# Where the ELU or sum of a one-head step stands on VectorE's queue, in a four-layer graph attention kernel

## The chip, the cores and the metric

The kernel runs on one core of one Trainium2 chip. The metric is the device time of one execution in microseconds (us). The engines are named as in the profile: PE is TensorE's matmuls, PEld its weight loads, DVE is VectorE, ACT is ScalarE, POOL is GpSimd, and SP is SyncE, whose queue issues all DMAs of the steady part of the run. L472 means line 472 of the kernel before.

## The reference

Sixteen graphs of 1024 nodes with 256 features go through four attention layers over one adjacency matrix. Every layer normalises x, takes the positive part, runs the layer and adds its result to x. Layers 0 and 2 have four heads of 64 features, layers 1 and 3 have one head of 256. Layers 0 to 2 end in an ELU, layer 3 in a plain positive part.

```python
h  = relu(layernorm(x))
Wh = h @ W                                    # per head
e  = leaky_relu(e_src[:, None] + e_dst[None]) # e_src, e_dst: Wh times two vectors
e  = where(adj > 0, e, -inf)
x  = x + elu(softmax(e, -1) @ Wh)             # layer 3: relu in place of elu
```

## The kernel before

**Steps.** A step is one layer of one graph. Four graphs are in flight at a time, and the function order_of_steps interleaves them, so that after the first steps a four-head step and a one-head step alternate. There are 64 steps, numbered n. Each step is cut into eight groups: for a four-head step two groups per head (four blocks of 128 rows each), for a one-head step one block of 128 rows per group. A group is one call of `aggregate` (64 matmuls of a weight tile with the projected features, L472), which ends with ACT copying the PSUM bank to y (L487).

**Weights.** For each head eight weight tiles w of 128 by 1024 are made on DVE by one instruction each (L455), from G (a broadcast row in PSUM), a column and the mask. The pool for w has 18 buffers (WBUFS). The 19th tile of a run of weights must wait until PE has used the first. Weights are emitted ahead of the matmuls: after each group up to six more tiles of a four-head step (`upto`), so a whole head and more may be queued on DVE before PE wants it.

**G.** For each step the column gcol is transposed on PE (L402), copied by ACT to gT (L404), stored to DRAM by SP (L406) and fetched back by SP as a broadcast row for each head (L430, gs). ACT copies gs to PSUM (L441, g).

**Preparation of a later step.** While step n-2 and n-1 run, the pieces of step n's preparation are emitted at planned places: statistics on DVE and POOL, the normalised rows on ACT (L334), a 16-bit split on ACT (L343), a DMA transpose on SP (L345), a merge on ACT (L351), the projection on PE (L376) with its copies by ACT (L378), two exponentials on ACT (L384, L386), the product on POOL (L388), and last gcol (L394, L395), gT and the store. The tuples FOUR, ONE and their like give for each of the 21 pieces the group at which it is emitted, counted from the first group of step n-2. A value of 11 is thus group 3 of the step before n. Entry 18 is the piece `rows`, which makes gT and stores it.

**The end of a step.** `finish(n)` returns pieces with the group of the next step at which each is to be emitted: `divide` (DVE, L508), `scaled` for each half (POOL, L519 and for an ELU L521), `exponential` for each half (ACT, L525, only for layers 0 to 2), `add` for each half (DVE, L531 and POOL, L532 for an ELU; DVE, L539 for layer 3) and, after layer 3, the stores of the output (L542). The list is called `ending` in the main loop. In a group k, pieces with a place below k are emitted ahead of the group's weights and matmuls, pieces with place k right after the matmuls, and then come the heads (`emit_heads`), the preparation pieces and the further weights:

```python
                while ending and ending[0][0] <= k:
                    ending.pop(0)[1]()
                upto = min(done["tiles"] + (6 if per > 1 else 3), done["free"] + WBUFS)
                emit_heads(upto - 1 + (C // 2 if per == 1 and k >= C - 2 else 0))
                if 8 * n + k in later:
                    later[8 * n + k]()
                prepare(8 * n + k)
                emit_tiles(upto)
```

[...] No scheduler reorders them. `slack(n)` says that the step after n has one head. A one-head step that is followed by a four-head step is one for which `slack(n)` is false. There are 29 such steps: 15 of layer 1 and 14 of layer 3.

Of the kernel before, what the change touches and what calls it, by code (L numbers as in the profile page):

```python
# [50 lines left out]
FOUR = (-8, -8, -5, 0, 1, 0, 3, 5, 5, 5, 5, 1, 4, 5, 5, 5, 5, 6, 8, 8, 10)  # L51
SHORT = (-4, -4, -4, 0, 1, 0, 3, 5, 5, 5, 5, 1, 4, 5, 5, 5, 5, 6, 8, 8, 10)
NEXT = (-4, -4, -4, 1, 3, 2, 5, 8, 8, 8, 8, 4, 7, 8, 8, 8, 8, 9, 10, 10, 12)
ONE = (2, 2, 2, 3, 4, 3, 5, 7, 7, 7, 7, 4, 7, 8, 8, 8, 8, 8, 11, 11, 12)
SOON = (0, 0, 0, 1, 2, 1, 3, 4, 4, 5, 5, 2, 5, 6, 6, 7, 7, 7, 8, 8, 10)
FIRST = (-4, -4, -4, -2, -0.9, -1, -1, -0.8, -0.8, -0.8, -0.8, 0, 0, 1, 1, 1, 1, 1, 2, 2, 4)
TIGHT = (4, 4, 4, 5, 6, 5, 7, 8, 8, 8, 8, 6, 8, 9, 9, 9, 9, 9, 10, 10, 12)
# [13 lines left out]
def kernel(ctx: ExitStack, tc: tile.TileContext, x, adj, ws, avs, out):  # L71
# [421 lines left out]
    def finish(n):  # L493

        b, l = steps[n]
        H = LAYERS[l][0]
        D = F // H
        st = state[n]

        def views(half):  # L500
            s = slice(half * HALF, (half + 1) * HALF)
            return (xs[b][:, s, :].rearrange("p c (h d) -> p (c h) d", h=H),
                    st["y"][:, s, :, 0:D].rearrange("p c h d -> p (c h) d"),
                    st["r"][:, s, :].rearrange("p c h -> p (c h)"))

        def divide():
            st["r"] = small.tile([P, C, H], F32, name="r")
            nc.vector.reciprocal(st["r"], st["y"][:, :, :, D])  # L508

        def scaled(half):  # L510
            xh, yh, r = views(half)
            rb = r[:, :, None].to_broadcast([P, HALF * H, D])
            if l < L - 1:

                e = st["e", half] = prep.tile([P, HALF * H, D], F32, name="rows",
                                                    bufs=HBUFS)
                if H > 1 and slack(n):
                    nc.vector.scalar_tensor_tensor(e, yh, 0.0, rb, op0=ALU.min, op1=ALU.mult)  # L518
            nc.gpsimd.tensor_tensor(yh, yh, rb, op=ALU.mult)  # L519
            if l < L - 1 and not (H > 1 and slack(n)):  # L520
                nc.gpsimd.tensor_scalar(e, yh, 0.0, -3.0e38, op0=ALU.min, op1=ALU.max)  # L521

        def exponential(half):
            if l < L - 1:
                nc.scalar.activation(st["e", half], st["e", half], AF.Exp)  # L525

        def add(half):
            xh, yh, r = views(half)
            if l < L - 1:
                e = st["e", half]  # L530
                nc.vector.scalar_tensor_tensor(e, e, -1.0, yh, op0=ALU.add, op1=ALU.max)  # L531
                nc.gpsimd.tensor_add(xh, xh, e)  # L532
                return
            if n == len(steps) - 4:

                nc.gpsimd.tensor_scalar(yh, yh, 0.0, 3.0e38, op0=ALU.max, op1=ALU.min)
                nc.gpsimd.tensor_add(xh, xh, yh)
                return
            nc.vector.scalar_tensor_tensor(xh, yh, 0.0, xh, op0=ALU.max, op1=ALU.add)  # L539

        def store(half):
            nc.sync.dma_start(  # L542
                out=out[b].rearrange("(p c) f -> p c f", p=P)[:, half * HALF:(half + 1) * HALF],
                in_=xs[b][:, half * HALF:(half + 1) * HALF, :])
            if half == 1 and b + STREAMS < B:
                load(b + STREAMS)

        if n == len(steps) - 3:

            def early(half):  # L550
                xh, yh, r = views(half)
                rb = r[:, :, None].to_broadcast([P, HALF * H, D])
                e = st["e", half] = prep.tile([P, HALF * H, D], F32, name="rows", bufs=HBUFS)
                nc.vector.scalar_tensor_tensor(e, yh, 0.0, rb, op0=ALU.min, op1=ALU.mult)  # L554
                if half == 0:
                    exponential(half)
                nc.vector.tensor_tensor(yh, yh, rb, op=ALU.mult)

            def late(half):
                xh, yh, r = views(half)  # L560
                e = st["e", half]
                nc.vector.scalar_tensor_tensor(e, e, -1.0, yh, op0=ALU.add, op1=ALU.max)
                nc.vector.tensor_add(xh, xh, e)

            def begin():
                divide()
                early(0)
                late(0)
                state[-1]["stats"](0)
                early(1)  # L570
                state[-1]["combined"](0)

            def end():
                late(1)
                state[-1]["stats"](1)
                state[-1]["combined"](1)

            return [(-1, begin), (1, lambda: exponential(1)), (1, end)]


        at = (0, 0, 0, 0, 1, 1, 1) if slack(n) and H > 1 else (0, 0, 1, 1, 2, 2, 3)
        return list(zip(at, (divide, lambda: scaled(0), lambda: scaled(1), lambda: exponential(0),
                             lambda: exponential(1), lambda: add(0), lambda: add(1)))) + (
                    [(4, lambda: store(0)), (4, lambda: store(1))] if l == L - 1 else [])
# [86 lines left out]
    with tc.manual_schedule():  # L671
        blocks = [mask_rows(c) for c in range(C)]
        layer = [weight_columns(l) for l in range(L)]
        layer[0][0](nc.scalar)
        load(0, 2)
        load_weights(0)
        for c in range(C):
            blocks[c][0]()
        load(1)
        load_weights(1)  # L680
        for i in range(2, STREAMS):
            load(i)
        for l in range(1, L):
            layer[l][0]()
        nc.scalar.activation(warm, half1, AF.Exp)
        nc.vector.tensor_copy(identb, ident)
        layer[0][1]()
        first = [piece for _, piece in preparation(0)]

        order = (  # L690

            [first[0], first[1], first[3], lambda: layer[0][2](range(1)), first[2],
             lambda: layer[0][2](range(1, K)), first[5], first[6], first[4], layer[0][3]]

            + [blocks[c][1] for c in range(4)]
            + [first[7], first[8], blocks[0][2], blocks[4][1], blocks[5][1], blocks[0][3],
               first[9], first[10], blocks[1][2], blocks[6][1], blocks[7][1], blocks[1][3],
               first[11], first[12], blocks[2][2], blocks[0][4],
               lambda: prepare(-4), first[13], first[14], blocks[1][4], blocks[2][3],
               blocks[3][2], first[15], first[16], blocks[3][3]]  # L700

            + [first[17], blocks[4][2], first[18], first[19], lambda: emit_heads(0),
               blocks[5][2], blocks[6][2], blocks[4][3], blocks[4][4], blocks[5][3], blocks[5][4],
               blocks[6][3], blocks[7][2], blocks[2][4], blocks[3][4], blocks[7][3],
               lambda: prepare(-2), blocks[6][4], lambda: prepare(-1), blocks[7][4]])
        plan(1)
        planned = 2
        done["prepared"] = 1
        for piece in order:
            piece()  # L710
        emit_tiles(C, must=True)
        prepare(-0.5)
        for i in range(2, STREAMS):
            load_weights(i)

        for l, at in ((1, 2), (2, 8 * 3 + 4), (3, 8 * 5 + 4)):
            for i, piece in zip((0, 1, 7), layer[l][1:]):
                later[at + i] = piece
        for n in range(len(steps)):
            for k, (h, i0, per) in enumerate(groups(n)):  # L720
                while planned < len(steps) and min(
                        a[0] for a in agenda_of[planned:planned + 2]) <= 8 * n + k:
                    plan(planned)
                    planned += 1
                while ending and ending[0][0] < k:
                    ending.pop(0)[1]()
                emit_tiles(place[n, h, C - 1] + 1, must=True)
                aggregate(n, h, i0, per)
                if i0 + per == C:
                    done["free"] = place[n, h, C - 1] + 1  # L730
# [5 lines that stand above are left out]
                if 8 * n + k in later:  # L736
                    later[8 * n + k]()
                prepare(8 * n + k)
                emit_tiles(upto)
            for _, piece in ending:  # L740
                piece()
            ending = finish(n) if n < len(steps) - 1 else []
# [35 lines left out]
```

## Time and profile before

| What | us |
|---|---|
| Median of three runs | 2445.25 (2444.63 to 2452.23) |
| The profiled execution's own time | 2449.74 |
| Its span, first to last instruction | 2448.0 |
| PE busy in that span | 2394.8 |
| DVE busy | 2040.0 |
| ACT busy | 1480.0 |
| POOL busy | 1073.7 |
| One pair of a four-head and a one-head step, 1373.96 to 1448.35 | 74.39 |

The page counts the time in which an engine works and the time in which it is idle, with what ended the idle time. The granted TensorE clock was 0.997 of full speed over the span. In the timeline of one engine a line has the start, the busy time, the engine, the source line, the operation, the tiles, and how many instructions were put together, and in square brackets the idle time ahead of it with the instruction that ended it. A wait on PE by DVE at L455 is a weight tile that waits for its buffer. A wait on ACT at L441 by DVE is one for G.

### The profile page before, as it was taken

How to read it: one execution, taken by the hardware profiler on the slowest of the kernel's cores; microseconds unless marked ns; L12 is line 12 of the kernel's file. 1: busy time of each engine (PE TensorE's matmuls, PEld its weight loads, DVE VectorE, ACT ScalarE, POOL GpSimd, SP SyncE). 2: the span in 40 equal slices, each digit the busy share in tenths (PEclk: the TensorE clock that was granted, in tenths of full speed). 3: DMA queues.
4: the chain of work that ended last, by engine and by line, in shares of the span. 5: the costliest groups of instructions: out<-in, count | busy, mean ns of one | idle time of the engine just before them, and what ended most of it. 6: DMA issues, size and time to landing. Idle time of an engine off the chain costs nothing.

```text
span 2448.0 us, 86681 instructions
## 1 busy us (share of the span) xinstructions
PE 2394.8 (98%) x39177; PEld 2153.2 (88%) x39177; DVE 2040.0 (83%) x2141; ACT 1480.0 (60%) x2505; POOL 1073.7 (44%) x1350
## 2 busy tenths in 40 slices
PE   7999999999999999999999999999999999999999
PEld 5888899899888888898998888888988998988987
DVE  8988588898888988887988888888889888888794
ACT  5465676565666656765656765566655577656542
POOL 3345455433345454544433554543443345545331
PEclk9999999999999999999999999999999999999999
DMA  5322233243333222323433322224334323223220
GB/s 182 83 53 63 45 79 67 66 114 92 85 96 79 72 63 52 74 71 96 114 89 88 80 62 71 64 50 108 75 93 114 95 48 80 68 65 76 75 54 35
DMA packets 292220, 191.84 MB, mean 78 GB/s; under 512 B 261778, under 2 KB 264586, under 8 KB 289930
## 3 DMA queue, kind: packets, MB, share of 16 engines
q1 hardware_dynamic: 291840, 186.29, 30.6%
q8 instruction: 307, 5.03, 0.9%
q14 instruction: 63, 0.52, 0.1%
q10 hardware_dynamic: 10, 0.00, 0.0%
HBM read 104.87 MB, written 17.43 MB: 50 GB/s over the span
## 4 chain that ended last, share of the span: by engine, by line
PE 82%; ACT 7%; DMA 5%; DVE 4%; issue 2%; POOL 0%; SPq 0%; DVEq 0%; ACTq 0%
PE bank L472 64%; PE bank L376 17%; DVE w L455 2%; DMA gs<-grow 2%; ACT rows L334 2%; DMA grow<-gT 2%; ACT g L441 1%; ACT rows L343 1%; ACT rows L525 1%; ACT rows L351 1%; ACT y L487 1%; DVE bn L287 1%; DMA rows<-rows 0%; PE bank L402 0%; ACT whx L378 0%
## 5 line engine op out<-in xcount | busy, mean ns | idle before, releaser
L472 PE MATMUL bank<-whx,w 128*64 128x65 f32 x36864 | 1898.0, 240 | 17.9 <-DVE w L455 9.3
L472 PEld LDWEIGHTS bank<-whx,w 128*64 128x64 f32 x36864 | 1745.7, 144 | 173.9 <-ACT whx L378 21.8
L455 DVE SCALAR_TENSOR_TENSOR w<-g,rcol,mask 128x1024 f32<-128x1024 f32 (+1 forms) x1288 | 1540.2, 1270 | 204.0 <-PE bank L472 165.2
L388 POOL TENSOR_TENSOR whx<-whx 128x1024 f32<-128x1024 f32 x128 | 244.5, 1910 | 819.1 <-ACT whx L386 819.1
L487 ACT ACTIVATE y<-bank 128x260 f32<-128x260 f32 (+1 forms) x504 | 192.1, 381 | 567.7 <-PE bank L472 567.7
L376 PE MATMUL bank<-wx,rows 128*128 128x264 f32 (+1 forms) x2048 | 484.8, 390 | 15.4 <-ACT y L487 11.8
L376 PEld LDWEIGHTS bank<-wx,rows 128*128 128x128 f32 x2048 | 380.9, 190 | 90.9 <-ACT y L487 17.9
L519 POOL TENSOR_TENSOR y<-y,r 128x1024 f32<-128x1024 f32 x124 | 259.0, 2098 | 222.0 <-DVE rows L518 188.4
L334 ACT ACTIVATE rows<-x,shift,rstd 128x256 f32<-128x256 f32 x512 | 265.2, 591 | 66.7 <-POOL shift L328 62.2
L378 ACT ACTIVATE whx<-bank 128x264 f32<-128x264 f32 (+1 forms) x512 | 193.7, 388 | 184.9 <-PE bank L376 184.6
L532 POOL TENSOR_TENSOR x<-x,rows 128x1024 f32<-128x1024 f32 x94 | 222.4, 2365 | 177.9 <-DVE rows L531 177.9
L351 ACT ACTIVATE rows<-rows 128x2048 uint16<-128x2048 uint16 x122 | 261.6, 2144 | 22.7 <-DMA rows<-rows 22.6
L343 ACT ACTIVATE rows<-rows 128x2048 uint16<-128x2048 uint16 x122 | 233.3, 1912 | 3.9
L531 DVE SCALAR_TENSOR_TENSOR rows<-rows,y 128x1024 f32<-128x1024 f32 x94 | 186.6, 1986 | 42.8 <-ACT rows L525 39.1
L287 DVE BATCH_NORM_STATS2 bn<-x 128x6 f32<-128x256 f32 x512 | 175.8, 412 | 34.5 <-POOL x L532 31.1
L441 ACT ACTIVATE g<-gs 128x1024 f32<-128x1024 f32 x158 | 161.8, 1024 | 67.1 <-DMA gs<-grow 55.9
L322 POOL TENSOR_TENSOR rstd<-rstd,neghalf 128x4 f32<-128x4 f32 (+1 forms) x97 | 121.3, 1251 | 41.1 <-DVE shift L323 33.8
L525 ACT ACTIVATE rows<-rows 128x1024 f32<-128x1024 f32 x96 | 100.7, 1048 | 4.2 <-DVE rows L554 4.2
L508 DVE RECIPROCAL r<-y 128x32 f32<-128x32 f32 (+1 forms) x63 | 17.4, 277 | 100.9 <-ACT y L487 100.9
L518 DVE SCALAR_TENSOR_TENSOR rows<-y,r 128x1024 f32<-128x1024 f32 x58 | 70.2, 1251 | 1.1
L386 ACT ACTIVATE whx<-whx,nbias 128x16 f32<-128x16 f32 (+1 forms) x128 | 40.4, 316 | 4.2
L384 ACT ACTIVATE rcol<-whx,rbias 128x16 f32<-128x16 f32 (+1 forms) x128 | 40.0, 313 | 4.2
(82 smaller groups left out, 461.9 us busy)
## 6 DMA issues: line engine op xcount, KB each, us to landing
gs<-grow SPq DMA_DIRECT2D x158, 512.0 KB
x<-in_x SPq DMA_DIRECT2D x15, 1024.0 KB
out<-x SPq DMA_DIRECT2D x30, 512.0 KB
w<-in_adj SPq DMA_DIRECT2D x8, 512.0 KB
rows<-rows SPq DMA_TRANSPOSE x122
x<-in_x SPq DMA_DIRECT2D x2, 512.0 KB
wx<-in_L_gnn_W SPq DMA_DIRECT2D x8, 128.0 KB
out<-x SPq DMA_DIRECT2D x8, 128.0 KB
```

The lines of the kernel that those rows point to most:

```text
L287: nc.vector.bn_stats(bn[:, c, :], xs[b][:, c, :])
L334: nc.scalar.activation(xn[:, :, q, :], xs[b][:, c, :].rearrange("p (k i) -> p k i", k=K), AF.Relu, bias=st["shift"][:, c:c + 1], scale=st[ ...
L343: nc.scalar.activation(bits, xn.rearrange("p (n s) -> p s n", s=2), AF.Copy)
L351: nc.scalar.activation(st["hT", half].rearrange("p k i -> p (k i)").bitcast(U16).rearrange("p (n s) -> p n s", s=2), st["turned", half].re ...
L376: nc.tensor.matmul(pw, lhsT=st["hT", half][:, k, q * P:(q + 1) * P], rhs=wx[l][:, k, :], start=(k == 0), stop=(k == K - 1))
L378: nc.scalar.activation(st["whx"][:, c, :], pw, AF.Copy)
L388: nc.gpsimd.tensor_tensor(wh[:, :, :, 0:D], wh[:, :, :, 0:D], wh[:, :, :, D:D + 1].to_broadcast([P, HALF, H, D]), op=ALU.mult)
L455: nc.vector.scalar_tensor_tensor(state[n]["w", h, j][:, s], state[n]["g", h][:, s], state[n]["rcol"][:, j, h:h + 1], masks[LAYERS[steps[n] ...
L472: nc.tensor.matmul(acc[o % P:o % P + cols, q, :], lhsT=st["w", h, jc][:, o:o + cols], rhs=st["whx"][:, jc, h * (D + 1):(h + 1) * (D + 1)], ...
L487: nc.scalar.activation(st["y"][:, i0:i0 + per, h, :], acc, AF.Copy)
L519: nc.gpsimd.tensor_tensor(yh, yh, rb, op=ALU.mult)
L532: nc.gpsimd.tensor_add(xh, xh, e)
```

## The change

Three things are changed.

1. For a one-head step that is followed by a four-head step, the pieces of its end get other places. `divide` stays at group 0. Both halves of `scaled` are emitted in group 0 (before: groups 0 and 1). Both halves of `exponential` get place 0.5 (before: groups 1 and 2). Both halves of `add` are emitted in group 1 (before: groups 2 and 3).
2. The main loop takes pieces with a place up to k + 0.5 once more, after the preparation pieces of the group and ahead of its further weights. Only the exponentials have such a place.
3. In the tuple ONE, entry 18 goes from 11 to 10: gT of a one-head step, and the issue of its store, are emitted one group sooner. Entry 19, which lets gs be fetched, stays at 11.

```diff
-ONE = (2, 2, 2, 3, 4, 3, 5, 7, 7, 7, 7, 4, 7, 8, 8, 8, 8, 8, 11, 11, 12)
+ONE = (2, 2, 2, 3, 4, 3, 5, 7, 7, 7, 7, 4, 7, 8, 8, 8, 8, 8, 10, 11, 12)
...
-        at = (0, 0, 0, 0, 1, 1, 1) if slack(n) and H > 1 else (0, 0, 1, 1, 2, 2, 3)
+        at = ((0, 0, 0, 0, 1, 1, 1) if slack(n) and H > 1 else
+              (0, 0, 0, 0.5, 0.5, 1, 1) if H == 1 and not slack(n) else (0, 0, 1, 1, 2, 2, 3))
         return list(zip(at, (divide, lambda: scaled(0), lambda: scaled(1), lambda: exponential(0),
                              lambda: exponential(1), lambda: add(0), lambda: add(1)))) + (
...
                 prepare(8 * n + k)
+                while ending and ending[0][0] <= k + 0.5:
+                    ending.pop(0)[1]()
                 emit_tiles(upto)
```

The order of the pieces in `at` is divide, scaled(0), scaled(1), exponential(0), exponential(1), add(0), add(1).

## The prediction

> **What bounds the kernel now.** I read the page's engine shares first, then the waits, then the timelines of one pair, always in the span of 2448.0 us.
>
> ```profile
> PE 2394.8 (98%) x39177; PEld 2153.2 (88%) x39177; DVE 2040.0 (83%) x2141; ACT 1480.0 (60%) x2505; POOL 1073.7 (44%) x1350
> ```
> PE is idle for only 53.2 us of the span, so PE sets the end. A change can gain only by closing PE's pauses, and any new pause of PE adds to the time in full. The waits say where the other engines have room (us in total, times, longest):
>
> ```profile
> DVE w L455 <- PE bank L472: 165.2, 30, 7.5
> ```
> ```profile
> PE bank L376 <- ACT y L487: 11.8, 14, 2.0
> ```
> DVE waits once per pair for weight buffers, about 5.5 us. That gap the change wants to fill. PE's largest repeated pause is at L376, behind an ACT that waits for G. In PE's timeline, weight loads included, ten such pauses from 656 us on sum to 10.5 us.
>
> Now a pair whose one-head step is of layer 1 (with ELU). I count from r, the start of its reciprocal (1373.96). DVE:
>
> ```profile
> 1373.96 0.20 DVE L508 RECIPROCAL r<-y 128x8 f32<-128x8 f32 x1
> 1374.07 6.01 DVE L455 SCALAR_TENSOR_TENSOR w<-g,rcol,mask 128x1024 f32<-128x1024 f32 x5
> 1385.65 7.24 DVE L455 SCALAR_TENSOR_TENSOR w<-g,rcol,mask 128x1024 f32<-128x1024 f32 x6 [5.57 <-PE bank L472]
> 1392.81 1.22 DVE L531 SCALAR_TENSOR_TENSOR rows<-rows,y 128x1024 f32<-128x1024 f32 x1
> 1393.94 2.47 DVE L455 SCALAR_TENSOR_TENSOR w<-g,rcol,mask 128x1024 f32<-128x1024 f32 x2
> 1396.33 1.26 DVE L531 SCALAR_TENSOR_TENSOR rows<-rows,y 128x1024 f32<-128x1024 f32 x1
> ```
> Five weights end at r+6.12. The gap is r+6.12 to r+11.69. The six weights after it complete head 2 and end at r+18.9. PE takes head 2 right after its L402:
>
> ```profile
> 1382.47 11.42 PE L472 MATMUL bank<-whx,w 128*64 128x65 f32 x384
> 1393.82 0.27 PE L402 MATMUL bank<-ident,gcol 128*8 128x128 f32 x1
> 1394.02 4.42 PE L472 MATMUL bank<-whx,w 128*64 128x65 f32 x144
> ```
> Three groups take 11.42 us, so one takes 3.78. Head 2 starts at r+20.06. Its first row block needs all eight weights within a quarter of a group, the eighth at about r+20.06 + 7/8 x 0.945 = r+20.89. The weights are ready only 2.0 us ahead of that. ACT, whose exponentials L531 reads:
>
> ```profile
> 1382.57 0.39 ACT L378 ACTIVATE whx<-bank 128x258 f32<-128x258 f32 x1 [0.48 <-PE bank L376]
> ...
> 1384.06 2.07 ACT L334 ACTIVATE rows<-x,shift,rstd 128x256 f32<-128x256 f32 x4
> 1386.16 1.91 ACT L343 ACTIVATE rows<-rows 128x2048 uint16<-128x2048 uint16 x1
> 1387.98 0.37 ACT L487 ACTIVATE y<-bank 128x260 f32<-128x260 f32 x1
> 1388.25 1.04 ACT L525 ACTIVATE rows<-rows 128x1024 f32<-128x1024 f32 x1
> ```
> The reader is to see that ACT copies projections until r+8.9, as PE delivers them, and is then busy without a gap to r+14.1 with preparation.
>
> [...] DVE idles 5.57 us ahead of a weight though later work is queued behind. [...] L531 takes 1.22 us here, with POOL idle, and up to 2.91 elsewhere.
>
> **Adds ahead of the waiting weights, layer 1.** The order as built is: DVE reciprocal, five weights, both L531, then 22 weights without a break. ACT, in group 0: the projection copies, L384, L386, L394, L395, L334 x4, L343, then both L525, then the copy y of group 1. So the exponentials are not early on ACT. They follow L343, where the first stood at r+14.3 already.
>
> POOL: L388 (r+2.2 to 4.1), then L519, L521, L519, L521 at 1.90, 1.04, 1.90, 1.04 us: both halves ready by r+10.1. That isn't what decides. ACT takes up the next instruction at r+14.02. Each L525 occupies it 0.95 (1.04, of which 0.09 overlaps): they end at r+15.07 and r+16.02. L531(0) runs r+15.1 to 16.34, L531(1) r+16.25 to 17.47, and the six weights start at r+17.38 instead of r+11.69. They end at r+24.62. PE's last weight of the first row block then runs at about r+24.68 instead of r+20.89: **PE pauses 3.79 us**. The slack of 2.0 us is counted in this.
>
> Is it recovered? Head 3's weights end near r+34.2, and PE wants them after its projections, near r+38.8; the next one-head weights near r+43.9, against r+47. So no second pause, and no recovery, for PE has no spare time: the pair is 3.79 us longer. At 851.37 head 2 already starts 0.64 late for want of instructions; there the addition is 3.15. The fourteen layer 1 steps with this layout (r = 331.34 to 2192.61) give 13 x 3.79 + 3.15 = 52.4 us. The first layer 1 step (r = 211.10) has no L334 and L343 ahead of its exponentials: six weights start some 2.5 us late, most within slack; I take 0.5 (-1 to 3).
>
> What the pause hides: pauses at L376 in these pairs, 0.83, 1.13, 0.34, 1.73, 0.44 and 0.64, sum 5.1. G's chain moves only by the 1.0 us by which two exponentials instead of one stand ahead of the second L343, PE comes 3.8 us later. I subtract 5.1.
>
> **Layer 3.** No exponentials. POOL's second L519 ends at about r+7.8. Both L539 read two SBUF tensors[...]: they end by r+10.2 at the latest, inside the gap that ends at r+11.69. Cover: DVE's wait for buffers. Head 3's weights come 2.2 us sooner, which PE doesn't need: 0 (-1 to 1). The moved L542 stores: none, their place is unchanged. Without that cover, two L539 would cost 2.4 us per pair.
>
> **Rows of G a group sooner.** L402 and L404 move; the store L406 keeps its place on SP, behind the second transpose.
>
> ```profile
> 1394.18 3.40 SPq L345 DMA_TRANSPOSE rows<-rows  x1
> 1397.64 0.47 SPq L406 DMA_DIRECT2D grow<-gT  x1
> ```
> gT was ready at 1395.80; L406 waited for the end of the L345 issue. In 27 of the 31 one-head stores L406 starts 0.04 to 0.09 after L345 ends, and in two 0.32 after. The other two have no L345 near; at 233.92 ACT doesn't wait for G at all. L345 itself waits for L343, which isn't moved. So the gain is 0 (0 to 0.3 us in two pairs). In the last (2360.76, r = 2340.24) gs comes 3.8 us sooner; but DVE reaches those weights only at 2368.8, after g at 2367.6: 0.
>
> **Sum.** 52.4 + 0.5 - 5.1 = +47.8 us, on the profiled execution 2449.74 to 2497.5. That execution is 4.5 above the median of the runs (2445.25); the difference is carried over to the median: **2493.0**.
>
> **The rivals.**
> - Faster. The exponentials reach ACT early enough and the gap takes all: then the six weights stay put and PE's pauses at L376 could go, 10.5 us, giving 2434.7. For: DVE's gap of 5.57. The point of decision: the second L525 must end by r+12.2 (16.02 less 3.79) for no loss. Against: L343 alone ends at r+14.1.
> - No change, 2445 to 2452: the six weights are late, but PE finds other work. Against: [...] head 2 is next.
> - Worse: POOL's L532(0) gets in ahead of L531(1), which then takes 2.69 (as at 1053.47) instead of 1.22: 14 x 1.47 = 20.6 more, 2513.6. For: L532(0) is released about when L531(1) starts. Against: L531(1) follows at once (0.09 overlap), and L532 starts 0.08 after its release.
> - The move of G does what it says and gains: excluded but for 0.3 us by SP's order.
>
> **How the numbers follow.** Forecast 0.85, worse 0.07, no change 0.04, faster 0.04. The forecast's own bounds: per pair 3.3 to 4.3 (7 us either way, for the release latencies that I took at 0.05), pauses kept or all gone (5.1 up, 5.4 down), first pair -1.5 to 2.5, layer 3 either way; not all at one end, 2484 to 2504. What lies outside is 0.15 and a twentieth of the forecast. About 0.3% (7.3 us) is what a measurement of this kernel can tell from no change. Faster 0.04, same 0.04, slower 0.92.
>
> **What would show it.** Right: layer 1 pairs about 77.5 us long, layer 3 pairs as before; in a layer 1 pair DVE waits at L531 for ACT L525 near 9 us, and a new wait of PE L472 for DVE w at head 2, some 3 to 4 us; L406 still behind L345. Wrong: DVE's L531 inside r+6 to r+12, or no PE pause at head 2.

## The result and the profile after

| What | before | after |
|---|---|---|
| Median of four runs each, us | 2446.68 (2444.63 to 2452.23) | 2508.91 (2507.89 to 2510.75) |
| The profiled execution's own time, us | 2449.74 | 2510.75 |
| Its span, us | 2448.0 | 2509.0 |
| Mean granted TensorE clock in that span | 0.997 | 0.987 |

The ratio of after to before is 1.0252, with a 95% interval of 1.0233 to 1.0271. The kernel is slower by 62.2 us, or by 61.0 us from profile to profile. The forecast was +47.8 us, and its range ended at 2504. So the direction held, and the size did not.

The first part of the page of after has the engines' busy time:

```profile
PE 2423.5 (97%) x39177; PEld 2179.3 (87%) x39177; DVE 2060.6 (82%) x2141; ACT 1480.4 (59%) x2505; POOL 1087.3 (43%) x1350
```

The number of instructions is the same on every engine. PE's idle time is 2509.0 - 2423.5 = 85.5 us, against 53.2 before, which explains 32 us of the 61. The other 28.7 us are in the busy time itself: PE needs longer for the same 39177 matmuls. A part of this is only how short groups are counted: in the timeline below, four matmuls between two pauses show 0.34 us, where four in a row take 0.12. The rest is the first sign of a cost that isn't a wait.

The waits of after show where the old wait of DVE went (us in total, times, longest):

```profile
DVE rows L531 <- ACT rows L525: 172.1, 47, 10.2
PE bank L472 <- DVE w L455: 49.0, 66, 0.9
DVE w L455 <- PE bank L472: 28.9, 15, 5.6
```

DVE's wait for weight buffers fell from 165.2 us in 30 pieces to 28.9 in 15. In its place stands a wait for the exponentials, 172.1 us. And PE now waits for weights, 49.0 us in 66 short pieces, against 9.3 in 12 before.

Now one pair with a layer 1 step, of the same place in the run as the one shown before. Its reciprocal starts at r = 1396.14. DVE in the timeline of after:

```profile
1396.14 0.19 DVE L508 RECIPROCAL r<-y 128x8 f32<-128x8 f32 x1
1396.25 6.00 DVE L455 SCALAR_TENSOR_TENSOR w<-g,rcol,mask 128x1024 f32<-128x1024 f32 x5
1411.21 2.36 DVE L531 SCALAR_TENSOR_TENSOR rows<-rows,y 128x1024 f32<-128x1024 f32 x2 [8.96 <-ACT rows L525]
1413.49 26.30 DVE L455 SCALAR_TENSOR_TENSOR w<-g,rcol,mask 128x1024 f32<-128x1024 f32 x22
```

The reader is to see a wait of 8.96 us between the five weights and the two adds. The six weights that complete head 2 stand behind the adds and start at r+17.35, where they started at r+11.69 before. ACT says why:

```profile
1406.23 2.06 ACT L334 ACTIVATE rows<-x,shift,rstd 128x256 f32<-128x256 f32 x4
1408.32 1.91 ACT L343 ACTIVATE rows<-rows 128x2048 uint16<-128x2048 uint16 x1
1410.14 1.99 ACT L525 ACTIVATE rows<-rows 128x1024 f32<-128x1024 f32 x2
```

The exponentials come after a later step's normalisation and split. ACT has no gap there, and the second exponential ends at r+15.99. PE pays:

```profile
1412.25 0.27 PE L402 MATMUL bank<-ident,gcol 128*8 128x128 f32 x1
1412.45 4.42 PE L472 MATMUL bank<-whx,w 128*64 128x65 f32 x144
1417.21 0.34 PE L472 MATMUL bank<-whx,w 128*64 128x65 f32 x4 [0.33 <-DVE w L455]
1418.40 0.34 PE L472 MATMUL bank<-whx,w 128*64 128x65 f32 x4 [0.86 <-DVE w L455]
1419.59 0.34 PE L472 MATMUL bank<-whx,w 128*64 128x65 f32 x4 [0.86 <-DVE w L455]
1420.78 8.44 PE L472 MATMUL bank<-whx,w 128*64 128x65 f32 x227 [0.85 <-DVE w L455]
```

PE walks along with DVE through the last weights: four pauses, which sum to 2.90 us, each ended by one weight. The 12 matmuls between them lie in 3.57 us (1417.21 to 1420.78), where 12 cost 0.36 us at the rate of 384 in 11.42. The last line is the surprise: 227 matmuls without a pause take 8.44 us, where that rate gives 6.75. The view by stretches shows the reason. Its columns are the stretch, its length, the busy time of PE, PEld, DVE, ACT and POOL with the number of instructions, the granted TensorE clock, the share of the DMA engines and GB/s:

```profile
1417.20:1421.30 4.10, 1.52 (x29) 1.11 (x30) 4.10 (x4) 2.79 (x5) 0.96 (x1) 1.00 0.77 133
1421.40:1424.80 3.40, 3.40 (x71) 3.40 (x67) 3.40 (x4) 0.00 (x0) 0.00 (x0) 0.50 0.44 142
1424.80:1428.20 3.40, 3.40 (x122) 3.40 (x122) 3.40 (x4) 2.66 (x3) 0.00 (x0) 1.00 0.05 17
```

For 3.4 us after the pauses the granted clock is 0.50. PE is fully busy, and the view lists 71 matmuls, where it lists 122 at full clock. This counts those already running when the stretch begins; 63 and 117 start within it. Over the span of after the clock is halved for 64.9 us in 16 stretches, against 13.7 us in 3 before. Thirteen of the 14 layer 1 pairs have such a stretch behind head 2's pauses, two of them a double one. The page's row of the clock doesn't show this: all its 40 slices read 9 before and after, because a slice is over 60 us long. The mean, 0.987 against 0.997, does.

The move of G is unchanged on SP's queue, in the timeline of after:

```profile
1417.33 2.65 SPq L345 DMA_TRANSPOSE rows<-rows  x1
1420.03 0.47 SPq L406 DMA_DIRECT2D grow<-gT  x1
```

The store L406 still starts 0.05 us behind the transpose's issue.

Summed over the 14 layer 1 pairs, the time goes from 1039.7 to 1102.6 us, +62.9. Everything else together is 1.9 us shorter. So the loss lies in these pairs.

### The profile page after: what moved, and what is told of

It reads as the page before. It is cut to its first block, busy times and chain, and to the rows that moved or that the text cites. A ratio compares the mean times of both kernels' runs of the same rounds, so it can differ in the third digit from the quotient of the medians.

```text
span 2509.0 us, 86681 instructions
## 1 busy us (share of the span) xinstructions
PE 2423.5 (97%) x39177; PEld 2179.3 (87%) x39177; DVE 2060.6 (82%) x2141; ACT 1480.4 (59%) x2505; POOL 1087.3 (43%) x1350
## 4 chain that ended last, share of the span: by engine, by line
PE 88%; DVE 5%; ACT 2%; issue 2%; DMA 2%; POOL 0%; SPq 0%; DVEq 0%; ACTq 0%
PE bank L472 70%; PE bank L376 18%; DVE w L455 4%; DMA gs<-grow 1%; DMA grow<-gT 1%; ACT rows L334 1%; DVE bn L287 0%; PE bank L402 0%; ACT rows L351 0%; ACT g L441 0%; ACT rows L343 0%; DVE rows L531 0%; DMA rows<-rows 0%; ACT y L487 0%; DVE mask L260 0%
## 5 line engine op out<-in xcount | busy, mean ns | idle before, releaser
L472 PE MATMUL bank<-whx,w 128*64 128x65 f32 x36864 | 1929.2, 243 | 58.7 <-DVE w L455 49.0
L472 PEld LDWEIGHTS bank<-whx,w 128*64 128x64 f32 x36864 | 1770.7, 146 | 218.7 <-DVE w L455 58.2
L388 POOL TENSOR_TENSOR whx<-whx 128x1024 f32<-128x1024 f32 x128 | 246.2, 1924 | 892.8 <-ACT whx L386 892.8
L376 PE MATMUL bank<-wx,rows 128*128 128x264 f32 (+1 forms) x2048 | 482.5, 390 | 7.0 <-ACT y L487 3.9
L376 PEld LDWEIGHTS bank<-wx,rows 128*128 128x128 f32 x2048 | 381.8, 191 | 81.5 <-ACT rows L351 9.6
L519 POOL TENSOR_TENSOR y<-y,r 128x1024 f32<-128x1024 f32 x124 | 258.4, 2098 | 222.0 <-DVE rows L518 188.4
L531 DVE SCALAR_TENSOR_TENSOR rows<-rows,y 128x1024 f32<-128x1024 f32 x94 | 184.9, 1980 | 175.7 <-ACT rows L525 172.1
L334 ACT ACTIVATE rows<-x,shift,rstd 128x256 f32<-128x256 f32 x512 | 264.5, 588 | 66.2 <-POOL shift L328 61.8
L532 POOL TENSOR_TENSOR x<-x,rows 128x1024 f32<-128x1024 f32 x94 | 235.3, 2510 | 142.8 <-DVE rows L531 142.8
L343 ACT ACTIVATE rows<-rows 128x2048 uint16<-128x2048 uint16 x122 | 233.2, 1911 | 3.9
L441 ACT ACTIVATE g<-gs 128x1024 f32<-128x1024 f32 x158 | 161.6, 1023 | 34.6 <-DMA gs<-grow 29.7
L539 DVE SCALAR_TENSOR_TENSOR x<-y,x 128x1024 f32<-128x1024 f32 x28 | 53.9, 1961 | 0.0
```

Source lines behind the costliest of these rows:

```text
L334: nc.scalar.activation(xn[:, :, q, :], xs[b][:, c, :].rearrange("p (k i) -> p k i", k=K), AF.Relu, bias=st["shift"][:, c:c + 1], scale=st[ ...
L343: nc.scalar.activation(bits, xn.rearrange("p (n s) -> p s n", s=2), AF.Copy)
L376: nc.tensor.matmul(pw, lhsT=st["hT", half][:, k, q * P:(q + 1) * P], rhs=wx[l][:, k, :], start=(k == 0), stop=(k == K - 1))
L388: nc.gpsimd.tensor_tensor(wh[:, :, :, 0:D], wh[:, :, :, 0:D], wh[:, :, :, D:D + 1].to_broadcast([P, HALF, H, D]), op=ALU.mult)
L472: nc.tensor.matmul(acc[o % P:o % P + cols, q, :], lhsT=st["w", h, jc][:, o:o + cols], rhs=st["whx"][:, jc, h * (D + 1):(h + 1) * (D + 1)], ...
```

## The experiments

My theory after the result: the whole loss is the layer 1 part, made of a pause of 3.8 us at head 2 and of a stretch of half clock that the pause triggers. One rival was that the pause itself is longer than forecast and the clock a companion without cost. Another was that layer 3 or the move of G take a share. A third question was whether a version gains from the gap that DVE has.

**One part alone: the rows of G.**

```diff
-ONE = (2, 2, 2, 3, 4, 3, 5, 7, 7, 7, 7, 4, 7, 8, 8, 8, 8, 8, 11, 11, 12)
+ONE = (2, 2, 2, 3, 4, 3, 5, 7, 7, 7, 7, 4, 7, 8, 8, 8, 8, 8, 10, 11, 12)
```

> Only entry 18 of ONE goes from 11 to 10. My theory (the store of G stays behind the second transpose on SP's queue): no change, within 3 us of the kernel before, and L406 still starts within 0.1 us of the end of an L345 in most pairs. Rival (a part of the 62 us comes from this move, or G sooner hides a gain of up to 10 us): slower by 5 to 15 us, or faster by up to 10.

Measured: 2445.57 against 2444.59, ratio 1.0005 (0.999 to 1.0021). No change. In 29 of the 31 one-head stores L406 starts 0.04 to 0.09 us behind the transpose L345.

**One part alone: the new places for layer 3 only.**

```diff
...
+              (0, 0, 0, 0.5, 0.5, 1, 1) if H == 1 and not slack(n) and l == L - 1 else (0, 0, 1, 1, 2, 2, 3))
...
```

> Only the layer 3 steps (no exponentials) get the new places; ONE and the layer 1 steps stay as before. My theory: both L539 fit into DVE's wait for buffers (r+6 to r+10, the six weights at r+11.7), no change, within 3 us of the kernel before, no pause of PE at head 2 and no stretch of half clock in these pairs. Rival (the adds on DVE as such cost time, or part of the 62 us is from these pairs): slower by 10 us or more. The intention of the change (a filled gap is a gain): faster by 5 us or more.

Measured: 2443.29 against 2444.59, ratio 0.9998 (0.9985 to 1.0011). No change, though the gap is used as intended. DVE in its timeline, in the pair whose reciprocal starts at 1074.41:

```profile
1080.44 3.98 DVE L539 SCALAR_TENSOR_TENSOR x<-y,x 128x1024 f32<-128x1024 f32 x2
1086.10 14.39 DVE L455 SCALAR_TENSOR_TENSOR w<-g,rcol,mask 128x1024 f32<-128x1024 f32 x12 [1.69 <-PE bank L472]
```

Both adds fill the gap, and 1.69 us of the wait for a buffer are left. The weights start when they did, since a buffer sets that and not DVE. PE waits for neither, so a filled gap of DVE is worth nothing here. In one point the expectation missed: this pair does have a stretch of half clock, at 1108.1 (the mean granted clock of the profile is 0.994). It stands not behind head 2 but behind a pause of 2.19 us at L376.

**One part alone: the new places for layer 1 only.**

```diff
...
+              (0, 0, 0, 0.5, 0.5, 1, 1) if H == 1 and not slack(n) and l < L - 1 else (0, 0, 1, 1, 2, 2, 3))
...
```

> Only the layer 1 steps get the new places; ONE and the layer 3 steps stay as before. My theory: the whole loss is here, 57 to 67 us slower than before, with L531 waiting for L525 near 9 us, a pause of PE at head 2, and 3.4 us of half clock in nearly every layer 1 pair. Rival (the parts share the loss): less than 50 us.

Measured: 2510.0 against 2444.59, ratio 1.0271 (1.0245 to 1.0296). That is the whole loss. PE's pauses at L472 for weights are 49.0 us in 65 pieces, and up to the last matmuls the clock is halved for 64.9 us in 16 stretches.

**Only the exponentials early, the adds at their old places.** Layer 3 and G stay as before.

```diff
...
+              (0, 0, 0, 0.5, 0.5, 2, 3) if H == 1 and not slack(n) and l < L - 1 else (0, 0, 1, 1, 2, 2, 3))
...
```

> In the layer 1 steps the scaling and both exponentials stand as early as in the changed kernel, but the two adds are left where they were before (groups 2 and 3). My theory (DVE held by an add that waits for ACT is the cause, not ACT's or POOL's new order): no pause at head 2, and at most what the second exponential ahead of L343 adds to the pauses at L376, 0 to 10 us slower than before. Rival (ACT's order is the cause: y of group 1 is copied 2 us later): 40 us slower or more.

Measured: 2451.46 against 2444.59, ratio 1.0027 (1.0016 to 1.0038). No pause at head 2 is left. So what costs is not where the exponentials stand on ACT but that the adds wait for them ahead of the weights. A loss of about 7 us remains. In its profile the pauses of PE at L376 for y are 13.1 us in 15, against 10.5 in 10 before (weight loads included), and up to the last matmuls the clock is halved for 23.9 us, against 13.7. Both point the right way, but neither was tried alone, and the clock is the weaker of the two: the trace of the kernel with layer 3 alone has 27.3 us of half clock, and its median shows no loss.

**The pause covered with unused matmuls.** After, with six matmuls whose result nobody reads, ahead of head 2 in the four-head steps that follow a layer 1 step.

```diff
+                if k == 4 and per > 1 and n and steps[n - 1][1] == 1:
+                    for _ in range(6):
+                        nc.tensor.matmul(bank(258), lhsT=ident, rhs=wx[1][:, 0, 0:258], start=True,
+                                         stop=True)
                 aggregate(n, h, i0, per)
```

> The changed kernel with six extra matmuls (128 by 128 by 258, about 0.46 us each, 2.8 us in all, their result unused) on PE ahead of head 2 of each four-head step that follows a layer 1 step. PE would otherwise stand still there, so the weights still end the group's start at the same moment. My revised theory (of the 62 us about 14 to 18 are from the granted clock that halves for 3.4 us after each pause): the stretches of half clock at head 2 go, and the time falls by 12 to 18 us against the changed kernel, to 2491 to 2497. Rival (the clock is only a symptom, the rest of the pair is longer for another reason): 2505 or more. Rival (extra matmuls simply add): 2520 or more.

Measured: 2491.2 against 2442.77, ratio 1.0194 (1.0168 to 1.022). That is 17.7 us less than after, by doing more work. Where each is compared with the kernel before as it ran beside it, the loss is 48.4 us in place of 62.2, so 13.8 us are won; by the profiled spans (2509.0 and 2487.8) it is 21.2. DVE in its timeline waits as in after:

```profile
1404.02 1.23 DVE L531 SCALAR_TENSOR_TENSOR rows<-rows,y 128x1024 f32<-128x1024 f32 x1 [8.94 <-ACT rows L525]
```

PE in the same timeline has the unused matmuls (L732) where the pauses were. The 0.46 us for one was an estimate from before: at L376 the 1024 records of this shape, two a matmul, are busy for 240.2 us. Here twelve records take 3.14.

```profile
1409.15 0.70 PE L732 MATMUL bank<-wx,ident 128*128 128x258 f32 x2
1410.40 2.44 PE L732 MATMUL bank<-wx,ident 128*128 128x258 f32 x10 [0.55 <-ACT y L487]
```

Then the same pair by stretches, first in the kernel with the six matmuls:

```profile
1388.97:1466.10 77.13, 76.58 (x1232) 68.57 (x1231) 62.95 (x66) 47.53 (x79) 37.43 (x44) 1.00 0.26 63
```

And in after:

```profile
1396.14:1474.87 78.73, 75.83 (x1220) 68.28 (x1219) 62.95 (x66) 47.43 (x79) 37.52 (x44) 0.98 0.25 62
```

Twelve more matmul records, and the pair is 1.60 us shorter. No layer 1 pair has half clock any more (the mean granted clock of the profile is 0.997). The shortest layer 3 pair in after, without pauses at head 2, takes 73.37. So the late weights alone cost 77.13 - 73.37 = 3.76 us a pair, and the half clock comes on top. The 14 layer 1 pairs sum to 1079.9 us here and to 1102.6 in after: 22.7 us for 15 stretches of 3.4 us, or 1.5 each. The rival of a clock without cost falls.

**Two unused matmuls in place of six.**

```diff
-                    for _ in range(6):
+                    for _ in range(2):
```

> The changed kernel with two extra matmuls (0.9 us) instead of six ahead of head 2. If the half clock follows only from a pause as long as the one seen (2.9 us of gaps), two already remove most stretches, and the time is 2491 to 2497 as with six. If it follows from the idle share of a wider stretch, the stretches stay and the time is 2503 to 2509.

Measured: 2501.4 against 2444.32, ratio 1.0233 (1.0217 to 1.025), between after and the six, so neither of the two forecast times came. Half clock is left in 5 of the 14 pairs (the mean granted clock of the profile is 0.993, where after has 0.987). So both kinds of pair stand in one run, and here they are neighbours by stretches:

```profile
1394.34:1471.46 77.12, 75.27 (x1224) 67.19 (x1223) 62.94 (x65) 47.46 (x79) 37.46 (x44) 1.00 0.31 64
1471.46:1550.18 78.72, 76.86 (x1224) 68.79 (x1223) 62.95 (x66) 47.49 (x79) 37.43 (x44) 0.98 0.25 63
```

The same instructions, the same weights' delay: 1.60 us more with one stretch of half clock. That is the price of a stretch, free of any change of code.

Why one pair and not the other? The pauses are the same in all 14 pairs (0.55, 0.45 and 0.85 us), so their length alone doesn't tell the five from the nine. What does was not shown.

**The exponentials ahead of the preparation on ACT.** After, with two places of FOUR and SHORT set to 0.25 and a second call of `prepare`, so that L334 and L343 follow the exponentials.

```diff
-FOUR = (-8, -8, -5, 0, 1, 0, 3, 5, 5, 5, 5, 1, 4, 5, 5, 5, 5, 6, 8, 8, 10)
-SHORT = (-4, -4, -4, 0, 1, 0, 3, 5, 5, 5, 5, 1, 4, 5, 5, 5, 5, 6, 8, 8, 10)
+FOUR = (-8, -8, -5, 0.25, 1, 0.25, 3, 5, 5, 5, 5, 1, 4, 5, 5, 5, 5, 6, 8, 8, 10)
+SHORT = (-4, -4, -4, 0.25, 1, 0.25, 3, 5, 5, 5, 5, 1, 4, 5, 5, 5, 5, 6, 8, 8, 10)
...
+                prepare(8 * n + k + 0.3)
                 emit_tiles(upto)
```

> The changed kernel, but the two exponentials stand ahead of L334 and L343 of the next preparation on ACT. My theory (the point of decision is the end of the second exponential, r+12.2): exponentials r+10.2 to 12.2, adds done by r+13.7, six weights from r+13.6 against a latest harmless start of r+13.6, so next to no pause at head 2 and no half clock; G comes about 1 us later in layer 1 pairs, so 0 to 10 us slower than before: 2446 to 2456. Rival (two adds ahead of the waiting weights cost DVE time wherever the exponentials stand): 2480 or more. Rival (the filled gap is a gain): below 2444.

Measured: 2456.3 against 2442.77, ratio 1.0049 (1.0031 to 1.0067). Of the loss of 62 us about 49 are gone. So the place behind L334 and L343, which the diff doesn't show, was what made the adds late. DVE in its timeline:

```profile
1383.86 2.94 DVE L531 SCALAR_TENSOR_TENSOR rows<-rows,y 128x1024 f32<-128x1024 f32 x2 [5.03 <-ACT rows L525]
```

And POOL:

```profile
1382.69 1.90 POOL L388 TENSOR_TENSOR whx<-whx 128x1024 f32<-128x1024 f32 x1
```

The first L531 takes 1.81 us, not 1.22, and starts while POOL's L388 runs. The six weights start at r+14.0. By the forecast's working no loss is paid up to r+13.6 (17.38 less 3.79), so the weights are 0.4 us late, and PE's pauses at head 2 are all below 0.25 us. A loss of some 13 us remains. At 0.4 us in each of 14 pairs up to 5.6 of it is the lateness. PE's pauses without a wait that the profile shows ("issue") are 10.7 us in 9, against 6.1 in 9 before, counting those above 0.25 us. The pauses at L376 are as before (9.8 us in 11).

**The store of G's row ahead of the transpose.** Before, with entries 18 and 19 of ONE at 9, so that L406 and L430 pass L345 on SP.

```diff
-ONE = (2, 2, 2, 3, 4, 3, 5, 7, 7, 7, 7, 4, 7, 8, 8, 8, 8, 8, 11, 11, 12)
+ONE = (2, 2, 2, 3, 4, 3, 5, 7, 7, 7, 7, 4, 7, 8, 8, 8, 8, 8, 9, 9, 12)
```

> The kernel before with entries 18 and 19 of ONE at 9: gT, its store and the fetch of gs are emitted ahead of the second split and its transpose, so that L406 and L430 pass that L345 on SP. My theory (G's chain is held by that L345, and ACT's wait for G is what makes PE pause at L376): L441 doesn't wait any more at this place, the pauses at L376 go, and the kernel is 5 to 11 us faster than before. Rival (the fetch then meets the other DMAs, or L430's waits hold back the second transpose and the merge): no change or slower.

Measured: 2455.37 against 2442.77, ratio 1.0051 (1.0033 to 1.0068): slower, and my theory missed. The pauses at L376 for y did go, from 10.5 us to 0. But in its waits of PE another line has grown, from 6.7 us in 12:

```profile
PE bank L472 <- issue: 26.6, 28, 2.1
```

PE stands still there for no wait that the profile shows. The fetch of gs (512 KB each) is now queued ahead of a transpose. That it delays PE's instructions is a guess; no run tells it apart.

**G's copy held back behind y.** Before, with the copy of G for the next one-head step (L441) kept out of groups 3 and 4, so that ACT first copies y, for which PE waits.

```diff
-            if n >= done["prepared"]:
+            if n >= min(done["prepared"], done["hold"]):
...
                 aggregate(n, h, i0, per)
+                done["hold"] = n + 1 if per > 1 and k in (3, 4) and slack(n) else 99
```

> The kernel before, but ACT copies y of group 5 ahead of L441 for the next one-head step (the G of that step is held back until group 5's matmuls are emitted). My theory (PE pauses at L376 because y stands behind an L441 that waits for gs): the pauses at L376, 10.5 us in the kernel before, fall to 3 us or less, DVE's one-head weights have 3.5 us of room, and the kernel is 4 to 10 us faster. Rival (as with the fetch ahead of the transpose, what is won at L376 comes back as PE waiting for its own instructions): no change or slower.

Measured: 2436.35 against 2444.32, ratio 0.9965 (0.9951 to 0.9979). This version beats both kernels, by some 8 us. The line of L376 waiting for y is gone from PE's waits, a new one of 3.0 us in 4 (L376 for whx) stands in its place, and the line of issue is about as before:

```profile
PE bank L472 <- issue: 7.6, 13, 2.1
```

**Both last ideas on after.** The kernel with the exponentials ahead of the preparation, and G's copy held back (the edits of both).

> The exponentials ahead of L334 and L343, and y of group 5 ahead of L441 as well. If what was left of the loss there (about 12 us) is the later G in layer 1 pairs, it falls by 5 to 10 us to 2446 to 2451. Rival (the loss is from elsewhere: the adds contend with POOL and the six weights start 0.4 us late, or PE waits for instructions): it stays within 3 us of 2456.

Measured: 2450.12 against 2444.32, ratio 1.0027 (1.0017 to 1.0036). It is 6 to 8 us better than without the hold (by the medians, and by the differences to before) and still slower than before. Against before with the hold, the early exponentials and adds still cost 13.8 us by the medians and 7.6 by the profiled spans (2446.1 and 2438.5). PE's waits differ by about as much as the latter: at L472 for weights 12.4 us against 7.8, and for issue 11.3 against 7.6, together 8.3. Why issue grows stays open, and so does the rest of the medians' difference; the profiled execution of before with the hold was the longest of its six.

## Why the prediction was right in its mechanism and too small in its size

- **The order on ACT and the adds: right.** Exponentials behind L334 and L343, L531 at 15.1 and 16.25 after r, the six weights at r+17.38 were forecast. The trace has 15.07, 16.21 and 17.35. DVE waits 8.96 us there ("near 9").
- **The weights' delay: right.** 3.79 us a pair was forecast (its 3.78 us for a group is the distance of the starts, 1382.47 to 1393.82, over three, and not 11.42 over three), the kernel with six unused matmuls shows 3.76, and the pair at r = 331.45, whose pause happened to leave the clock alone, is 3.88 longer than before.
- **"So no second pause, and no recovery, for PE has no spare time: the pair is 3.79 us longer": this step failed.** There is no second pause, but the same matmuls run slower after the first. A stretch of 3.4 us at half clock follows in 13 of 14 pairs, twice a double one. It costs 1.6 us in neighbouring pairs of one run, and 22.7 us over the run. A pair with one stretch takes 78.5 to 79.0 us in place of the forecast "about 77.5"; 77.1 is what it takes where six unused matmuls keep half clock away. The sum had no term for it.
- **The trace of before had shown it.** Four pauses for weights of 0.85 us each, at 242 to 246 us, are followed by the same thing, here in the view by stretches of before:

```profile
242.90:246.50 3.60, 1.03 (x14) 0.62 (x14) 3.60 (x4) 3.57 (x7) 3.42 (x5) 1.00 0.42 79
246.60:250.00 3.40, 3.40 (x66) 3.40 (x68) 3.38 (x9) 3.40 (x4) 1.04 (x6) 0.50 0.56 105
250.00:253.40 3.40, 3.40 (x122) 3.40 (x120) 3.40 (x4) 1.65 (x2) 2.94 (x7) 1.00 0.64 118
```

  The prediction priced a pause and not what follows one. No long pause stood ahead of the half clock: PE was busy for 1.03 us of 3.60 here and for 1.52 of 4.10 in the pair of after, and no pause in either is above 0.86.
- **The pauses that vanish: too small, by 7.** I took off 5.1 us, those at L376 alone. Without half clock the 14 pairs would have grown by 1079.9 - 1039.7 = 40.2 us, where the sum had 52.4 - 5.1 = 47.3. In the trace of before PE stands still for 7.6 us in these pairs, 1.9 of them without a cause that the profile shows. And a pause costs more than it shows: those of 2.90 us at head 2 cost 3.76. Whether this makes up the whole 7.1 stays open. So the miss of 15.6 us in these pairs is +22.7 for the clock and -7.1 for this. The second hid a part of the first.
- **The first layer 1 pair: within its range.** +0.5 us (-1 to 3) was forecast; it went from 88.47 to 88.34.
- **Layer 3 and the rows of G: right,** both nothing, and each alone was run. The forecast that both L539 lie within the gap holds (r+6.03 to r+9.99). The first takes 2.82 us in the pair of after at r = 561.12, where an L539 in before takes 1.22; POOL's L519 runs for 1.74 us of it. That L519 is the cause is an estimate from this overlap.
- **The rival "worse", 2513.6, came near the time by the wrong road.** It had L531(1) at 2.69 us. In these pairs it takes 1.22. Its time being close is no evidence for it.
- **The rival "faster"** needed the second exponential by r+12.2. With the exponentials ahead of the preparation it ended at r+12.06 (1384.77, with r = 1372.71). The first add then took 1.81 us in place of 1.22, with POOL's L388 running as it began, the weights came at r+14.0, and the kernel was still slower than before by 0.49% (0.31 to 0.67). DVE's gap was no resource that PE lacked.

## What to carry to other kernels

In this kernel a pause of TensorE, which bounds it, had two prices: its length, and the half clock that followed (1.6 us a stretch). It followed four pauses of 0.33 to 0.86 us, 2.90 in all; so add up pauses that stand close together, don't take the longest alone, and read the granted clock just behind similar pauses in the trace of before. Where an engine has an idle gap ahead of an instruction that waits for a buffer, ask first what the work put there must itself wait for, on its own engine's queue as built and not as the diff reads; here it waited longer than the buffer did. The gain lay elsewhere: ordering the copy for which PE waits ahead of one for which it doesn't gave 0.35% (0.21 to 0.49).

## What the runs showed of the hardware that was not expected

- Half clock came behind short pauses with work between them, in 13 of 14 pairs after some 2.9 us of pauses, and in 5 of 14 with part of them filled. In after PE is busy for 0.85 to 1.60 us of the 3.41 us just ahead of the half clock in the 13 pairs. The 14th, at 331.45, has the same pauses (0.34, 0.86, 0.85 and 0.86 us), and the clock behind them stays at 1.00: its 228 matmuls take 7.20 us, where the 227 above took 8.44. What sets it apart was not shown.
- At half clock 63 matmuls started in 3.4 us against 117 at full clock, 46% less. So a stretch that is full of work loses 1.6 us of its 3.4, as the neighbouring pairs do.
- More work made the kernel faster: six unused matmuls a pair took off 13.8 us by the differences to before, and 21.2 by the profiled spans.
- The spread between runs of one kernel goes with the clock. Of 43 runs of before on one chip, 7 with a mean clock of 0.994 or 0.995 average 2450.2 us, and 15 with 0.997 or 0.998 average 2442.8. On two other chips the same groups average 2448.3 and 2442.0 (27 runs), and 2445.6 and 2443.8 (11 runs). What makes the clock differ from run to run was not tried.
